# Scan layer: centring y from the first direction on, and ScalarE copying y into the opened PSUM sum

## Chip, cores and metric

The kernel runs on one core of one Trainium2 chip. The metric is the device time of one execution in microseconds (us). In this document TensorE is PE in the profile, its weight loads PEld, VectorE is DVE, ScalarE is ACT, GpSimd is POOL and the sync engine is SP.

## What is computed

Four layers run one after the other on 8 images of 64 channels and 64 x 64 pixels. Only the first, the scan layer, is touched. Per image it normalises and projects the input, convolves it, and runs a selective scan over the 4096 pixels in four directions k (along rows, along columns, and both backwards) with 16 states n per inner channel:

```python
def step(h, inp):
    u_t, dt_t, B_t, C_t = inp
    h = h * jnp.exp(dt_t[..., None] * A) + dt_t[..., None] * B_t[:, :, None, :] * u_t[..., None]
    return (h, jnp.einsum('bkcn,bkn->bkc', h, C_t))
...
y = out_y[:, 0] + inv[:, 0] + wh + invwh
y = _ln(y, outnorm_g, outnorm_b, LN_EPS) * jax.nn.silu(z)
```

Each `out_y` also has `D * xs` added, which is the input u scaled by channel. y is the sum of the four directions. `_ln` subtracts the mean over the 128 inner channels, and divides by the root of the variance.

## The kernel before, in words

`scan_layer` keeps the 128 inner channels on the partitions and cuts the 4096 pixels into 4 chunks of 1024 (`CH`), each two PSUM banks of 512 (`BK`) wide. An image is 16 steps: 4 directions by 4 chunks. The document numbers them by place, 0 to 15. All 8 images make 128 steps in one stream. A step is 16 units, one for each state n.

A unit is made of these instructions, in calls that run ahead of one another:

- `load` (L729, queued on SP) brings the row of C for this state, spread over 128 partitions, into a `ct` buffer (5 buffers). For units 0, 3, 6 and 8 (`BY_POOL`) the row of B comes likewise into `bt`.
- `decay` (L733): ScalarE's exponential a, 3 buffers.
- `spread`: z in PSUM (2 buffers). For the units in `BY_POOL` POOL multiplies bt (L741) and ScalarE copies it to PSUM (L748); for the other 12 TensorE spreads a bf16 row by two products (L751), and DVE multiplies (L778).
- DVE's scan h (L782, 3 buffers), then POOL's product of ct with h, in place in ct (L787).
- `sum_up` (L848): TensorE adds ct into the sum `yps`, two products of 512 columns in f32. The program's weights for this are `ctl["mat"]`: the identity up to place 10, and `lno_cen` (identity less 1/128 everywhere, which takes off the mean over channels) from place 11 on.

Sums come 3 units late (`LAG`). The instruction order on every engine is written out by hand in the loop over n at the end of `scan_layer`: `empty`, `spread(n + 1)`, then at n = 3 `bg.before` and `begin_sum`, at other n `sum_up` (twice at n = 7) and `bg.before`; then the loads, `decay(n + 2)`, `save_state` (L769, ScalarE copies one column), `product`, `unit(n)`, and `bg.after`. `bg` is the background queue: it interleaves the normalisation, projections and convolution (L544) of other steps and images, one piece per unit. `bg.before` issues the TensorE part of a piece, `bg.after` first all that was handed to `bg.later`, then the evacuation of the piece before (L647 and L648, for example).

The sum `yps` has one buffer of two banks. When the last unit of a step has been added, `empty` (L817), at n = 3 of the next step, lets ScalarE copy the sum to y in SBUF, and `begin_sum` opens the next one:

- at places 0 to 3 (`new_y`) by a product of u with `skipd`, the diagonal of the summed D;
- at places 4 and 12 the sum of the place before is kept (the direction turns on the same chunk), and nothing is opened;
- at the other ten by a product of the y that is there with `ctl["mat"]` (L839).

So 80 of the 128 steps open their sum from y: the "y steps". At the last four places the weights `lno_cen` centre both the y that is read back and the last direction, so that y is centred when `norm_y` takes its squares.

Of the kernel before, what the change touches and what calls it, by code (L numbers as in the profile page):

```python
# [11 lines left out]
BF16 = mybir.dt.bfloat16  # L12
AF = mybir.ActivationFunctionType
ALU = mybir.AluOpType
# [8 lines left out]
BK = 512  # L23
NBK = L // BK
DI = 128
N = 16
R = 4
CH = 1024
NCH = L // CH
# [212 lines left out]
def scan_layer(cm, x_in, w, xh):  # L242

    tc, nc = cm.tc, cm.nc
    with ExitStack() as ctx:
# [34 lines left out]
        for k in range(4):  # L280
# [5 lines left out]
            ps = psum.tile([128, BK], F32, name="wps", tag="mm")  # L286
# [14 lines left out]

        skip = cm.tile([DI, 1], "skip")
        nc.vector.tensor_reduce(skip, dcol, AX.X, ALU.add)
        skipd = cm.tile([DI, DI], "skipd")
        nc.vector.tensor_scalar(skipd, cm.ident, skip, None, ALU.mult)
        ln1_cen, ln1_avg = cm.tile([2 * C, 2 * C], "ln1_cen"), cm.tile([2 * C, 2], "ln1_avg")
        nc.vector.memset(ln1_cen, 0.0)
        nc.vector.memset(ln1_avg, 0.0)
# [6 lines left out]
            ln1_row, cm.ident[:NBK, :NBK].unsqueeze(2).to_broadcast([NBK, NBK, C])  # L315
        )
        lno_cen, lno_avg = cm.norm_consts(DI, "lno")

        eps = cm.tile([128, 1], "eps")
        nc.vector.memset(eps, 1e-5)  # L320
# [3 lines left out]
            rows, cm.ident[: 3 * N, : 3 * N].rearrange("p (i n) -> p n i", n=N), AX.X, ALU.add  # L324
        )
        nc.vector.tensor_copy(pick, rows)
        pad = padp.tile([DI, S + 2, S + 2], F32, name="pad", tag="pad")
        nc.gpsimd.memset(pad, 0.0)
        bg = Background()
# [272 lines left out]
        def ordered(t, k, c):  # L602

            if k % 2 == 0:
                return t[:, bass.ts(c, CH)].rearrange("p (a b) -> p a b", b=S)
            q = CH // S
            return t.rearrange("p (h w) -> p w h", w=S)[:, c * q : (c + 1) * q, :]
# [73 lines left out]
        def pieces(ctl, low):  # L681

            by_place = "a n (j x) -> (n j) a x"

            def fetch():
                low["b"] = work.tile([128, 2, 128], F32, name="bw", tag="bw", bufs=1)
                nc.sync.dma_start(low["b"], low["bc"][:, :N].rearrange(by_place, x=128))

            def first():
                low["p"] = work.tile([128, 3, 2, 128], BF16, name="bp", tag="bp", bufs=1)  # L690
                nc.scalar.copy(low["p"][:, 0], low["b"])

            def subtract():
                low["r"] = work.tile([128, 2, 128], F32, name="br", tag="br", bufs=1)
                nc.gpsimd.tensor_tensor(low["r"], low["b"], low["p"][:, 0], ALU.subtract)

            def second():
                nc.scalar.copy(low["p"][:, 1], low["r"])

            def third():  # L700
                nc.gpsimd.tensor_tensor(low["p"][:, 2], low["r"], low["p"][:, 1], ALU.subtract)

            def store():
                low["bsd"] = dr.tile([2, 3 * N, CH], BF16, name="bsd", tag="bsd", bufs=8)
                for i in range(3):
                    nc.sync.dma_start(
                        low["bsd"][:, i * N : (i + 1) * N].rearrange(by_place, x=128),
                        low["p"][:, i],
                    )

            def get():
                ctl["bs"] = work.tile([3 * N, CH], BF16, name="bs", tag="bs")
                nc.sync.dma_start(ctl["bs"], low["bsd"][ctl["k"] // 2])

            return ([fetch, first, subtract, second, third, store] if ctl["k"] < 2 else []) + [get]
# [77 lines left out]
        def layout(b, name):  # L793

            im = images[b]
            if name not in im:
                first = ("row", "col")[steps(b)[0][0] % 2]
                if name != first:
                    bg.flush(b - 1)
                at = b % 2 if name == first else 1 - b % 2  # L800
                im[name] = io.tile([DI, L], F32, name="y", tag=f"y{at}", bufs=1)
            return im[name]

        def own(t, c):
            return t[:, bass.ts(c, CH)].rearrange("p (a b) -> p a b", b=S)
# [18 lines left out]
        def begin_sum():  # L824


            ctl = pending[0][0]
            if kept:
                ctl["ps"] = kept.pop()
                return  # L830
            ctl["ps"] = psy.tile([DI, CH], F32, name="yps", tag="yps")
            half = BK // S
            if ctl["new_y"]:
                wt, so = skipd, ordered(ctl["u"], ctl["k"], ctl["c"])
            else:
                mine = ("row", "col")[ctl["k"] % 2]
                wt, so = ctl["mat"], own(layout(ctl["b"], mine), ctl["c"])
            for i in range(CH // BK):
                nc.tensor.matmul(  # L839
                    ctl["ps"][:, bass.ts(i, BK)].rearrange("p (a b) -> p a b", b=S),  # L840
                    wt, so[:, i * half : (i + 1) * half, :], start=True, stop=False,
                )

        def sum_up():

            ctl, n, ct = pending.popleft()
            for i in range(CH // BK):
                nc.tensor.matmul(  # L848
                    ctl["ps"][:, bass.ts(i, BK)], ctl["mat"], ct[:, bass.ts(i, BK)],
                    start=False, stop=(n == N - 1 and not ctl["turns"]),  # L850
                )
            if n == N - 1:
                if ctl["turns"]:
                    kept.append(ctl["ps"])
                else:
                    full.append(ctl)

        def steps(b):


            out = []
            for k in (0, 2, 1, 3) if b < NB - 1 else (1, 3, 0, 2):
                cs = range(NCH) if k < 2 else range(NCH - 1, -1, -1)
                out += [(k, c, i) for i, c in enumerate(cs)]
            return out
# [3 lines left out]
        def prepare(b, s):  # L869

            if b not in images:
                return None
            u = images[b]["u"]
            k, c, i = steps(b)[s]
            ks = [steps(b)[q * NCH][0] % 2 for q in range(4)] + [0]
            q = s // NCH
            bg.finish(b, 2 * c + 2 if s < NCH and k == 0 else NBK)
            low = lows.setdefault((b, k % 2, c), {}) if k < 2 else lows.pop((b, k % 2, c))
            dt, ut, e, items, soft = project(u, k, c, low)
            if b == 0 and s < NCH:  # L880
                items = later.pop(s, []) + items + [(None, soft[0]), (None, soft[1])]
            bg.add(items, first=True)
            new = work.tile([DI, N], F32, name="state", tag="state", bufs=3)
            ctl = dict(
                b=b, k=k, c=c, u=u, into=("row", "col")[ks[q + q % 2]], dt=dt, bc=low["bc"][k // 2], ut=ut, dus=e, soft=soft, new=new, state=None,
                first=(i == 0), new_y=(s < NCH), turns=(s % (2 * NCH) == NCH - 1),
                mat=lno_cen if s >= 3 * NCH - 1 else cm.ident,
            )
            ctl["pieces"] = pieces(ctl, low)
            return ctl  # L890
# [20 lines left out]
        with tc.manual_schedule():  # L911
            start(0)
            bg.drain()
            ctl = prepare(0, 0)
            bg.drain()
            ctl["soft"][2]()
# [10 lines left out]
            for b in range(NB):  # L927
                for s in range(4 * NCH):
# [3 lines left out]
                    if s + 1 < 4 * NCH:  # L932
                        nxt = prepare(b, s + 1)
                    else:
                        nxt = prepare(b + 1, 0)
# [22 lines left out]
                    for n in range(N):  # L958
# [3 lines left out]
                        if n == LAG + 1:  # L962
                            bg.before(n in idle, slots)
                            begin_sum()
                        else:
                            if len(pending) > LAG:
                                sum_up()
                            if n == LAG + 5:
                                sum_up()
                            bg.before(n in idle, slots)  # L970
# [22 lines left out]
                        if late and n == LAG + 2:  # L993
                            c = 4 * NCH - s
# [7 lines left out]
                    ctl = nxt  # L1002
            save_state()
            while pending:
                sum_up()
# [1152 lines left out]
```

## Time and profile before

| what | us |
|---|---|
| median of 3 runs (12318.48 to 12333.17) | 12329.48 |
| the profiled execution | 12328.75 |
| its span, first to last instruction | 12326.7 |
| first scan begins, last scan ends | 94.4, 7018.6 |
| POOL ct L787, 2048 instructions | 4794.6 busy, 2364 ns each |
| TensorE sums L848, 8192 records | 630 ns mean each |
| openings from y L839, 320 records | 592 ns median each |
| mean granted TensorE clock | 0.952 |

A row of groups reads: line, engine, operation, output and inputs by name, shape, count; then busy time in us and mean ns of one; then the engine's idle time just before these instructions, and what ended it. A product in f32 shows as two records of MATMUL, two passes; so 4096 sums of 512 columns are 8192 records. TensorE's records overlap their successors, so its busy share is no measure of how full it is. In a timeline the first two columns are start and duration, and square brackets hold the idle time before the instruction and what ended it. A row of waits gives us in total, times, and the longest.

### The profile page before, as it was taken

How to read it: one execution, taken by the hardware profiler on the slowest of the kernel's cores; microseconds unless marked ns; L12 is line 12 of the kernel's file. 1: busy time of each engine (PE TensorE's matmuls, PEld its weight loads, DVE VectorE, ACT ScalarE, POOL GpSimd, SP SyncE). 2: the span in 40 equal slices, each digit the busy share in tenths (PEclk: the TensorE clock that was granted, in tenths of full speed). 3: DMA queues.
4: the chain of work that ended last, by engine and by line, in shares of the span. 5: the costliest groups of instructions: out<-in, count | busy, mean ns of one | idle time of the engine just before them, and what ended most of it. 6: DMA issues, size and time to landing. Idle time of an engine off the chain costs nothing. (4 is left out here: it accounts for less than half of the span.)

```text
span 12326.7 us, 120038 instructions
## 1 busy us (share of the span) xinstructions
PE 11203.1 (91%) x38827; PEld 4075.9 (33%) x38827; DVE 10359.2 (84%) x7334; ACT 7820.8 (63%) x10409; POOL 7399.3 (60%) x3510
## 2 busy tenths in 40 slices
PE   7899999999999999999998899999987779999999
PEld 2233332332332332333322233232335463333333
DVE  5999999999999999999999776868677686676767
ACT  4776776776766766767766554646547574555554
POOL 5999999999999999999999700000006480000000
PEclk8999999999999999999999899999998789999999
DMA  3666666666666666666666400000011100000000
GB/s 115 207 213 218 209 209 217 219 203 216 218 210 213 211 210 217 213 215 213 199 213 211 164 24 26 5 25 7 17 41 41 41 21 24 19 4 19 5 11 6
DMA packets 541331, 1562.16 MB, mean 127 GB/s; under 512 B 127360, under 2 KB 144400, under 8 KB 538128
## 3 DMA queue, kind: packets, MB, share of 16 engines
q1 hardware_dynamic: 540688, 1554.36, 38.5%
q8 instruction: 309, 5.06, 0.2%
q14 instruction: 334, 2.74, 0.1%
HBM read 1456.41 MB, written 88.87 MB: 125 GB/s over the span
## 5 line engine op out<-in xcount | busy, mean ns | idle before, releaser
L787 POOL TENSOR_TENSOR ct<-ct,h 128x1024 f32<-128x1024 f32 x2048 | 4794.6, 2364 | 248.2 <-DVE h L782 113.3
L782 DVE TENSOR_TENSOR_SCAN h<-a,state,z 128x1024 f32<-128x1024 f32 x1536 | 3573.1, 2342 | 118.2 <-ACT z L748 67.1
L1159 DVE TENSOR_TENSOR sum<-sum,ex 128x1024 f32<-128x1024 f32 x1920 | 2347.5, 1223 | 618.1 <-ACT ex L1152 484.4
L1152 ACT ACTIVATE ex<-sc 128x1024 f32<-128x1024 f32 x2048 | 1968.1, 1024 | 1359.6 <-PE sc L1147 1359.6
L848 PE MATMUL yps<-ct,ident 128*128 128x512 f32 x5632 | 2809.0, 630 | 2.5 <-POOL ct L787 2.4
L733 ACT ACTIVATE a<-dt,amat 128x1024 f32<-128x1024 f32 x2048 | 2345.4, 1147 | 725.9 <-DVE h L782 712.5
L778 DVE TENSOR_TENSOR z<-z,e 128x1024 f32<-128x1024 f32 x1536 | 1863.3, 1213 | 221.1 <-PE z L751 143.2
L1166 PE MATMUL av<-ex,v 128*64 128x512 f32 x8192 | 1950.0, 604 | 0.0
L1147 PE MATMUL sc<-q,k 16*128 16x512 f32 (+1 forms) x8192 | 1562.2, 623 | 4.2 <-ACT q L1140 3.1
L848 PEld LDWEIGHTS yps<-ct,ident 128*128 128x128 f32 x5632 | 1006.4, 194 | 1384.2 <-issue 1220.6
L751 PE MATMUL z<-bs,pick 48*128 48x512 bf16 x3072 | 948.0, 389 | 536.5 <-DVE h L782 485.5
L848 PE MATMUL yps<-ct,lno_cen 128*128 128x512 f32 x2560 | 1276.3, 630 | 0.0
L782 DVE TENSOR_TENSOR_SCAN h<-a,z 128x1024 f32<-128x1024 f32 x512 | 1162.7, 2282 | 81.4 <-ACT z L748 57.2
L741 POOL TENSOR_TENSOR bt<-bt,e 128x1024 f32<-128x1024 f32 x512 | 1210.1, 2364 | 5.3 <-DMA bt<-bc 5.3
L1473 POOL TENSOR_TENSOR gt<-gt,pad 128x1024 f32<-128x1024 f32 x16 | 34.9, 2179 | 1570.2 <-ACT gt L1472 1570.2
L1166 PEld LDWEIGHTS av<-ex,v 128*64 128x64 f32 x8192 | 512.2, 136 | 1332.8 <-issue 1278.9
L1147 PEld LDWEIGHTS sc<-q,k 16*128 16x128 f32 (+1 forms) x8192 | 528.4, 184 | 1016.2 <-issue 977.3
L748 ACT COPY z<-bt 128x1024 f32<-128x1024 f32 x512 | 519.8, 1015 | 537.5 <-POOL bt L741 334.8
L751 PEld LDWEIGHTS <-pick 48*128 48x128 bf16 x3072 | 177.6, 95 | 1754.9 <-DVE h L782 1003.0
L848 PEld LDWEIGHTS yps<-ct,lno_cen 128*128 128x128 f32 x2560 | 458.1, 193 | 618.3 <-issue 564.2
L544 PE MATMUL vps<-pad,convd 128*128 128x512 f32 x1152 | 550.9, 602 | 12.9 <-ACT e L648 12.9
L1846 DVE RECIPROCAL r<-e 128x512 f32<-128x512 f32 x128 | 420.7, 3323 | 0.0
(416 smaller groups left out, 10449.5 us busy)
## 6 DMA issues: line engine op xcount, KB each, us to landing
ct<-bc SPq DMA_DIRECT2D x2048, 512.0 KB
bt<-bc SPq DMA_DIRECT2D x512, 512.0 KB
x<-x SPq DMA_DIRECT2D x12, 2048.0 KB
bc<-e SPq DMA_DIRECT2D x128, 128.0 KB
zd<-z SPq DMA_DIRECT2D x64, 256.0 KB
z<-zd SPq DMA_DIRECT2D x64, 256.0 KB
x<-x SPq DMA_DIRECT2D x32, 512.0 KB
part<-x SPq DMA_DIRECT2D x128, 128.0 KB
```

Of the source, the lines that this page charges most:

```text
L544: nc.tensor.matmul(held[0].rearrange("p (r c) -> p r c", c=S), convd[:, t, :], pad[:, j * rows + dy : (j + 1) * rows + dy, dx : dx + S], s ...
L733: ctl["exp", n] = nc.scalar.activation(ctl["a", n], ctl["dt"], AF.Exp, scale=amat[:, ctl["k"], n : n + 1])
L741: nc.gpsimd.tensor_tensor(bt, bt, ctl["dus"], ALU.mult)
L751: nc.tensor.matmul(z[:, bass.ts(i, BK)], pick[:, n : n + 1].to_broadcast([3 * N, DI]), ctl["bs"][:, bass.ts(i, BK)], start=True, stop=True,)
L778: first = nc.vector.tensor_tensor(z, z, ctl["dus"], ALU.mult)
L782: nc.vector.tensor_tensor_scan(h[:, flip], a[:, flip], z[:, flip], 0.0 if state is None else state[:, n : n + 1], ALU.mult, ALU.add,)
L787: freed[at] = nc.gpsimd.tensor_tensor(ct, ct, h, ALU.mult)
L848: nc.tensor.matmul(ctl["ps"][:, bass.ts(i, BK)], ctl["mat"], ct[:, bass.ts(i, BK)], start=False, stop=(n == N - 1 and not ctl["turns"]),)
L1147: nc.tensor.matmul(sc[:, e, :], k[r : r + d, bass.ts(j, 128)], qs[i][r : r + d, :], start=True, stop=True,)
L1152: nc.scalar.activation(ex, sc, AF.Exp)
L1159: nc.vector.tensor_tensor(sums[i], sums[i], ex, ALU.add)
L1166: nc.tensor.matmul(avs[i][r, :], v[:, j, r], ex[:, e, :], start=(j == 0), stop=(j == TQ - 1))
```

## The change

y is centred by every sum, not only from place 11 on: `skipd` is now the centring matrix times the summed D, `sum_up` always has the weights `lno_cen`, and `ctl["mat"]` is gone. What a y step reads back is therefore centred already and needs no product. Such a step opens its two banks with two products of a bf16 row of zeros (`nil`, 1 partition by 512), which make 128 x 512 zeros each, and ScalarE then copies y, 128 x 1024 f32, from SBUF over them. The copy is handed to `bg.later`, so it is issued at the end of n = 3, after the exponential of unit 5 and `save_state`. The sums that follow add to it.

```diff
-        skipd = cm.tile([DI, DI], "skipd")
-        nc.vector.tensor_scalar(skipd, cm.ident, skip, None, ALU.mult)
...
         lno_cen, lno_avg = cm.norm_consts(DI, "lno")
+        skipd = cm.tile([DI, DI], "skipd")
+        nc.vector.tensor_scalar(skipd, lno_cen, skip, None, ALU.mult)
...
+        nil = cm.pool.tile([1, BK], BF16, name="nil", tag="nil")
+        nc.vector.memset(nil, 0.0)
...
-            if ctl["new_y"]:
-                wt, so = skipd, ordered(ctl["u"], ctl["k"], ctl["c"])
-            else:
+            if not ctl["new_y"]:
                 mine = ("row", "col")[ctl["k"] % 2]
-                wt, so = ctl["mat"], own(layout(ctl["b"], mine), ctl["c"])
+                y = layout(ctl["b"], mine)
+                for i in range(CH // BK):
+                    nc.tensor.matmul(
+                        ctl["ps"][:, bass.ts(i, BK)], nil[:, :DI], nil, start=True, stop=False
+                    )
+                bg.later(lambda: nc.scalar.copy(ctl["ps"], y[:, bass.ts(ctl["c"], CH)]))
+                return
+            so = ordered(ctl["u"], ctl["k"], ctl["c"])
             for i in range(CH // BK):
                 nc.tensor.matmul(
                     ctl["ps"][:, bass.ts(i, BK)].rearrange("p (a b) -> p a b", b=S),
-                    wt, so[:, i * half : (i + 1) * half, :], start=True, stop=False,
+                    skipd, so[:, i * half : (i + 1) * half, :], start=True, stop=False,
                 )
...
-                    ctl["ps"][:, bass.ts(i, BK)], ctl["mat"], ct[:, bass.ts(i, BK)],
+                    ctl["ps"][:, bass.ts(i, BK)], lno_cen, ct[:, bass.ts(i, BK)],
...
-                mat=lno_cen if s >= 3 * NCH - 1 else cm.ident,
```

## The prediction, made before the result was known

> **What bounds the kernel now.** I began with the page's busy table and its 40 slices.
>
> ```profile
> PE 11203.1 (91%) x38827; PEld 4075.9 (33%) x38827; DVE 10359.2 (84%) x7334; ACT 7820.8 (63%) x10409; POOL 7399.3 (60%) x3510
> PE   7899999999999999999998899999987779999999
> DVE  5999999999999999999999776868677686676767
> ACT  4776776776766766767766554646547574555554
> POOL 5999999999999999999999700000006480000000
> ```
>
> POOL's digits are nines in the first 22 slices alone: that is the scan layer. Its first scan starts at 94 us and its last ends at 7018.6, so 128 steps take 54.1 us each. Nothing outside it changes. Next, the groups of instructions restricted to 94 to 7020 us, and the waits of the same stretch.
>
> ```profile
> L787 POOL TENSOR_TENSOR ct<-ct,h 128x1024 f32<-128x1024 f32 x2048 | 4794.6, 2364 | 248.2 <-DVE h L782 113.3 <-DMA ct<-bc 79.0 <-PE dps L619 16.6
> L778 DVE TENSOR_TENSOR z<-z,e 128x1024 f32<-128x1024 f32 x1536 | 1863.3, 1213 | 221.1 <-PE z L751 143.2 <-POOL ct L787 24.5 <-ACT u L553 15.1
> L748 ACT COPY z<-bt 128x1024 f32<-128x1024 f32 x512 | 519.8, 1015 | 537.5 <-POOL bt L741 334.8 <-DVE h L782 170.1 <-DVE z L778 14.9
> ...
> PEld yps L839 <- ACT y L817: 58.6, 72, 2.6
> ```
>
> By the stretch table POOL is busy 6676 of those 6926 us (96%), DVE 6549, ScalarE 4899. POOL is the bound; only its idle time can be won. I sorted its gaps over 0.06 us by unit and by kind of step. The 80 steps that open their sum from y (places 5 to 11 and 13 to 15 of each image's 16; in places 4 and 12 the sum is kept, 0 to 3 open from u) hold 125 us of POOL idle, 100 of it ahead of units 4 to 9. Why there, the timeline of one such step (place 14 of the third image) shows:
>
> ```profile
> 2630.06 0.19 ACT L769 COPY state<-h 128x1 f32<-128x1 f32 x1
> 2630.41 1.88 PE L839 MATMUL yps<-y,lno_cen 128*128 128x512 f32 x4
> 2632.22 0.60 PE L751 MATMUL z<-bs,pick 48*128 48x512 bf16 x2
> 2632.75 1.98 PE L848 MATMUL yps<-ct,lno_cen 128*128 128x512 f32 x4
> 2632.96 1.23 DVE L778 TENSOR_TENSOR z<-z,e 128x1024 f32<-128x1024 f32 x1 [0.48 <-PE z L751]
> 2638.58 2.36 POOL L787 TENSOR_TENSOR ct<-ct,h 128x1024 f32<-128x1024 f32 x1 [0.85 <-DMA ct<-bc]
> 2642.09 2.37 POOL L787 TENSOR_TENSOR ct<-ct,h 128x1024 f32<-128x1024 f32 x1 [1.16 <-DMA ct<-bc]
> ```
>
> The opening product (L839), z of unit 5 (L751), the first sum (L848), and then sums and convolution pieces follow on TensorE without a gap for 16 us. A sum releases its ct buffer; the load of a later ct waits for that buffer; POOL waits for the load. So in these steps TensorE's place in time after the opening is POOL's idle time. Place 9 agrees: the same step of different images takes 51.9 us where the opening begins 0.5 us after scan 3's end, 53.5 at 2.0, and 54.9 at 3.5.
>
> **What the skill says.** "PSUM — Partial Sum Buffer", section on the matmul accumulator, rule 2: ScalarE's writes leave the has_written bits alone, and a matmul without the first flag adds only where the bit is set. That is why two matmuls by zeros must open the banks; no trace here tests it. "TensorE: Matmul & The Clock Gate", Part 1: the clock is full or half, decided in free-running windows of 3.413 us. The trace agrees: in the scan the granted clock takes only the values 1 and 0.5, changes on a grid of 3.413 us, and is at half for 452 us. I set each window's streaming time beside the next window's clock: of 86 full-clock windows streaming under 45%, 81 were followed by half clock; of those over 60%, one of 1693. "ScalarE: Activation LUTs", section on what a table load costs: an immediate-scale activation takes 186 ns + 0.833 ns per element, 1039 ns for 1024, against 1015 in the L748 row.
>
> **Part by part, per y step.**
>
> TensorE loses 2 f32 products of 512 columns. Each is two passes, 0.43 us start to start in the timeline: 4 x 0.43 = 1.71 us. It gains two bf16 products of 1 row by 512 columns. Not in the trace; nearest is z (48 rows, 512 columns, bf16), 0.23 us start to start. Bounds 0.21 and, at half clock, 0.43 each; I take 0.22, so 0.43 for both, and 0.65 until the result is seen (0.60 for the z pair in its row, plus a semaphore). z of unit 5, queued behind, comes 1.28 us earlier unless scan 3 still holds its buffer.
>
> ScalarE gains one 128x1024 copy from SBUF to PSUM: the L748 row is that shape and direction, 1.015 us; bounds 1.0 and 1.15 (the L733 exponential). 80 x 1.03 = 82 us on ScalarE. It stands in its queue behind the exponential of unit 5 and state copy of unit 2 (L769), ahead of the background's evacuation (L647, L648 in that step) and the exponential of unit 6. It waits for the zero products; meanwhile those instructions wait too. Cover: after L769, ScalarE's idle time up to unit 8's z copy plus that copy's lead over scan 8 is 2.3 to 8.6 us in the 80 steps; copy and wait need 1.03 (1.9 or less in nine of ten, 4.1 at most), and the least margin is 0.8 us. For unit 6, reckoned alike, it is 0.15. So zero; if that cover were gone the copies would cost up to 82 us.
>
> **The added wait.** The first sum (L848) now waits for the copy. Behind it on TensorE stand the background product, sums 1 and 2, z of unit 7, the double sum; all that POOL's loads wait for. So the first sum's new start is the later of z 5 issued (opening + 0.95) and copy done + 0.06, with copy done = later of (L769's end, opening + 0.65) + 1.03. In the step shown: the opening starts at 2630.41, so the copy would end at 2630.41 + 0.65 + 1.03 = 2632.09 and the sum start at 2632.15 instead of 2632.75: 0.60 earlier. I did this for all 80 steps, and set against it what POOL idled ahead of units 4 to 9, since POOL can't gain more than it idles (means of 8 images, us):
>
> ```
> place      5    6    7    8    9    10   11   13   14   15
> advance   1.50 0.40 0.60 0.60 0.56 0.61 0.71 0.56 0.71 0.52
> POOL idle 0.87 0.26 0.50 0.43 0.77 0.93 3.25 1.59 1.94 1.95
> smaller   0.70 0.08 0.22 0.13 0.25 0.35 0.67 0.53 0.67 0.44
> ```
>
> "Smaller" is taken step by step before averaging. It sums to 32.5 us; the advances alone to 54. What is late next where the stall shrinks is the same ct load, only less, or POOL's own work.
>
> **The rest.** The sums of places 0 to 10 change weights from ident to lno_cen: 630 ns in both rows, 0. skipd is built a few DVE instructions later and nil is a memset of 512 elements on one partition; DVE idles 12.3 us soon after, before its reciprocal, and skipd is first used at 104.6 us: 0. No DMA is moved. SP's and POOL's orders are untouched.
>
> **Sum.** The profiled execution took 12328.75 us (span 12326.7 and 2.05 around it), within 0.8 us of the median, 12329.48. 12329.5 - 32.5 = 12297.
>
> **Rivals.**
>
> *POOL's work hides it.* POOL is busy 96%, and an earlier ct load may only uncover the next limit: DVE's results, of which it waits 113 us in the scan, or unit 9's load behind the double sum. For it: places 6 to 8 show next to no reachable idle. Against: places 11 to 15 wait 0.85 to 1.7 us for DMA several times in a row. If a quarter remains: -8 us, 12321.
>
> *Half clock* (the other side). The opening loses 1.28 us of streaming, 37% of a window, and TensorE now idles between z 5 and the copy's end. A window that falls under about 45% halves the next: 3.41 us streaming half as much, 1.71 us late, in just those sums POOL waits for. For it: place 5 already has 1.3 such windows per step, all y steps 0.36; whether products of one row count as activity no row shows. Against: shifting the grid over the streaming times with the change put in, I find 0.20 steps with a low window against 0.18, since background products fill TensorE right before the opening. It decides from 32.5 / 1.71 = 19 more such windows on. With 40, half a window per step: +68 - 32.5 = +36, 12365.
>
> *ScalarE comes late.* If z 8 or the step size (L653, L656) is late by half the copy in each step: +41 - 32.5 = +9, 12338. Against: the cover above.
>
> **Chances.** Forecast 0.58 (12275 to 12316), POOL hides it 0.21, half clock 0.15, ScalarE 0.06. About 0.2% (25 us) is what a measurement can tell from no change. Of the forecast's 0.58 some 0.45 lies beyond 25 us, with 0.02 of the others: faster 0.47. Slower is half clock and a little of ScalarE: 0.16. The rest, 0.37, is within. Range: below, all advances count (54) and some half windows vanish (about 12): 12263; above, into the half-clock case at about 30 windows, +20: 12350; some 0.08 of chance lies beyond each end.
>
> **What would show it.** Right: in the y steps POOL's idle ahead of units 4 to 9 falls from 100 us to about 68; DVE's wait for z L751 (143 us) falls; the new copies take about 1.03 us; the first sum waits for the copy 0.5 to 1 us in most steps; half clock stays near 452 us. Wrong: half clock over 500 us; POOL idle unchanged though the first sums are earlier; a new DVE wait for ScalarE's z or a.

## The result, and the profile after

The changed kernel takes 12349.25 us (median of 20 runs), against 12332.27 for the kernel before in the same number of runs: a ratio of 1.0015, 95% interval 1.001 to 1.0021. That is about 18 us slower, where 32 us faster was forecast: inside the stated range of 12263 to 12350 us, but on the wrong side of no change, which the interval excludes. Of all executions below one, of e9, ran in a much slower state (25855 us, mean granted clock 0.481), and no ratio counts it.

Executions of one kernel scatter, those of the changed kernel from 12330 to 12373 us, so one profile shows better where time goes than how much. The profiled execution of the changed kernel has a span of 12347.8 us, and its scan layer alone is 25 us longer than in the profile before: the last scan ends at 7044.0 us, not 7018.6.

The code after has moved down by two to seven lines: POOL's product is L789, the sums L855, DVE's z product L780, ScalarE's z copy L750. New are the zero products L839 and the copy L842. From the page of the changed kernel, the busy table and the slices:

```profile
PE 11169.4 (90%) x38667; PEld 4050.9 (33%) x38667; DVE 10362.7 (84%) x7335; ACT 7890.5 (64%) x10489; POOL 7398.9 (60%) x3510
POOL 5999999999999999999999800000006480000000
```

POOL's own work is the same to a microsecond, so the added time is POOL's idle time. The groups of the changed kernel between 94 and 7045 us:

```profile
L789 POOL TENSOR_TENSOR ct<-ct,h 128x1024 f32<-128x1024 f32 x2048 | 4791.1, 2360 | 274.4 <-DVE h L784 129.2 <-DMA ct<-bc 85.2 <-PE z L753 19.6
L855 PE MATMUL yps<-ct,lno_cen 128*128 128x512 f32 x8182 | 4144.3, 638 | 61.3 <-ACT yps L842 57.0 <-POOL ct L789 4.3
...
L780 DVE TENSOR_TENSOR z<-z,e 128x1024 f32<-128x1024 f32 x1536 | 1864.3, 1214 | 234.4 <-PE z L753 138.4 <-POOL ct L789 24.1 <-ACT state L771 15.6
...
L842 ACT COPY yps<-y 128x1024 f32<-128x1024 f32 x80 | 81.5, 1018 | 28.7 <-PE yps L839 27.7
```

The first row's idle time has risen from 248.2 to 274.4 us, though TensorE has less to do. The last row is the copy as it was costed: 1.018 us, 81.5 in all. The second row has the added wait, 57.0 us, and one more thing: a sum's record lasts 638 ns on average where it lasted 630. The median is 592 ns in both, so more of the sums ran at half clock. The granted clock says the same: in the scan it is at half for 602 us, not 452; over the whole profile it is 0.946, not 0.952. This is no accident of two profiles: the mean clocks of the 20 executions of the changed kernel lie between 0.943 and 0.948, those of 147 executions of the kernel before, timed beside the experiments, between 0.950 and 0.955. Behind the scan the clock is at half for 673 to 701 us in all 15 profiles, so it is in the scan that they differ. A step of 0.001 in the mean clock is 25 us of half clock.

What half clock costs at a bad spot, the start of place 7 in the fourth image shows. In the 17 us up to this point TensorE's instructions stand in the same order in both kernels, at the same distances to 0.02 us; only the edges of the windows fall elsewhere. First the changed kernel in the table of stretches, cut on the grid of 3.413 us:

```profile
3109.50:3112.91 3.41, 2.91 (x5) 1.04 (x6) 3.41 (x4) 2.34 (x4) 3.41 (x3) 0.50 0.65 227
3112.92:3116.32 3.40, 3.40 (x6) 0.87 (x5) 3.37 (x3) 1.81 (x3) 3.40 (x2) 0.50 0.13 49
3116.33:3119.74 3.41, 3.41 (x5) 0.96 (x4) 3.38 (x3) 2.18 (x3) 3.05 (x2) 0.50 0.27 102
```

The third number from the right is the clock: half, three windows long. The same units in the kernel before:

```profile
3102.77:3106.18 3.41, 3.41 (x6) 0.60 (x4) 3.37 (x4) 2.34 (x5) 3.41 (x2) 0.50 0.19 71
3106.18:3109.59 3.41, 3.41 (x8) 1.17 (x8) 3.37 (x3) 1.74 (x4) 3.41 (x3) 1.00 0.57 178
```

One window, then full clock. The changed kernel's timeline shows what follows at the opening of this step:

```profile
3116.65 0.34 PEld L855 LDWEIGHTS yps<-ct,lno_cen 128*128 128x128 f32 x1 [0.52 <-issue]
...
3122.55 1.92 ACT L819 COPY y<-yps 128x512 f32<-128x512 f32 x2 [1.34 <-PE yps L855]
...
3125.03 0.60 PE L839 MATMUL yps<-nil 1*128 1x512 bf16 x2
3125.73 1.02 ACT L842 COPY yps<-y 128x1024 f32<-128x1024 f32 x1 [0.24 <-PE yps L839]
3126.89 1.95 PE L855 MATMUL yps<-ct,lno_cen 128*128 128x512 f32 x4 [0.72 <-ACT yps L842]
3128.10 2.36 POOL L789 TENSOR_TENSOR ct<-ct,h 128x1024 f32<-128x1024 f32 x1 [1.10 <-DVE h L784]
```

The weight load of 0.34 us, 0.19 at full clock, is the sign of half clock. ScalarE's emptying copies wait 1.34 us for the last sum of the step before, everything behind them is late, and POOL idles. Place 7 takes 56.1 us after and 53.8 before (means of images 2 to 7); places 5, 9 and 11 take 0.6 to 1.0 us less than before.

The zero products of this step are not what makes these three windows: they come later, at 3125.03 us. The length of place 7 goes with where a window's edge falls. In the changed kernel, e3 and e12 (below) ten of these 18 steps are longer than 55 us, and those ten alone begin between 0.2 us before an edge and 0.6 us behind one. The changed kernel has five of them, e3 two, e12 three, the kernel before one. So a part of what this profile lost, 2.3 us in each of six steps, may be the chance of one execution; what the zero products themselves do to the clock, e3 shows.

### The profile page after: what moved, and what is told of

Its sections match the earlier page's. It is cut to its first block, busy times and chain, and to the rows that moved or that the text cites. A ratio compares the mean times of both kernels' runs of the same rounds, so it can differ in the third digit from the quotient of the medians.

```text
span 12347.8 us, 119848 instructions
## 1 busy us (share of the span) xinstructions
PE 11169.4 (90%) x38667; PEld 4050.9 (33%) x38667; DVE 10362.7 (84%) x7335; ACT 7890.5 (64%) x10489; POOL 7398.9 (60%) x3510
## 5 line engine op out<-in xcount | busy, mean ns | idle before, releaser
L789 POOL TENSOR_TENSOR ct<-ct,h 128x1024 f32<-128x1024 f32 x2048 | 4791.1, 2360 | 274.4 <-DVE h L784 129.2
L855 PE MATMUL yps<-ct,lno_cen 128*128 128x512 f32 x8192 | 4148.6, 638 | 61.3 <-ACT yps L842 57.0
L1158 ACT ACTIVATE ex<-sc 128x1024 f32<-128x1024 f32 x2048 | 1967.9, 1024 | 1359.8 <-PE sc L1153 1359.8
L855 PEld LDWEIGHTS yps<-ct,lno_cen 128*128 128x128 f32 x8192 | 1487.4, 196 | 2101.6 <-issue 1829.0
L780 DVE TENSOR_TENSOR z<-z,e 128x1024 f32<-128x1024 f32 x1536 | 1864.3, 1214 | 234.4 <-PE z L753 138.4
L750 ACT COPY z<-bt 128x1024 f32<-128x1024 f32 x512 | 519.7, 1015 | 499.8 <-POOL bt L743 295.8
L1855 POOL TENSOR_TENSOR r<-r,half 128x512 f32<-128x512 f32 x128 | 162.7, 1271 | 362.1 <-issue 188.0
L771 ACT COPY state<-h 128x1 f32<-128x1 f32 x2048 | 361.5, 177 | 4.7 <-DVE h L784 4.7
```

What stands on the lines that cost most here:

```text
L780: first = nc.vector.tensor_tensor(z, z, ctl["dus"], ALU.mult)
L789: freed[at] = nc.gpsimd.tensor_tensor(ct, ct, h, ALU.mult)
L855: nc.tensor.matmul(ctl["ps"][:, bass.ts(i, BK)], lno_cen, ct[:, bass.ts(i, BK)], start=False, stop=(n == N - 1 and not ctl["turns"]),)
L1158: nc.scalar.activation(ex, sc, AF.Exp)
```

## The experiments

Each was timed in alternation with the kernel before; ratios are to that kernel. "Half clock" is the sum over the scan in the profiled execution, where three kernels with the same TensorE work for the opening (before, e1, e2) gave 452, 476 and 435: differences under 40 us say nothing.

**e1, the centring alone.** `skipd` is centred as in the change; the other edits are:

```diff
...
-                wt, so = ctl["mat"], own(layout(ctl["b"], mine), ctl["c"])
+                wt, so = cm.ident, own(layout(ctl["b"], mine), ctl["c"])
...
-                mat=lno_cen if s >= 3 * NCH - 1 else cm.ident,
+                mat=lno_cen,
```

> Only the centring: every sum has the weights lno_cen and skipd is centred, but the y steps open by a product with the identity as before; no zero products, no ScalarE copy, no new wait. Clock theory (the zero products of one row and TensorE's new waits leave windows with too little activity, so the clock is halved more often): none of that is here, so half clock in the scan stays near 452 us and the time near the kernel before, 12332 +- 8 us. Weights theory (dense weights in all sums cost something): 12349 us, with half clock near 602.

Measured: 0.9996 (0.9988 to 1.0004), 12327 us, half clock 476. No cost of the dense weights shows.

**e2, ScalarE's load alone.**

```diff
+            if not ctl["new_y"]:
+                y = layout(ctl["b"], mine)
+                idle_copy = work.tile([DI, CH], F32, name="idle_copy", tag="idle_copy", bufs=1)
+                bg.later(lambda: nc.scalar.copy(idle_copy, y[:, bass.ts(ctl["c"], CH)]))
```

> The kernel before with one thing added: in each y step ScalarE makes the same 128x1024 copy of y at the same place of its queue, but into an SBUF tile that nobody reads; the opening product stays on TensorE. ScalarE theory (82 us more on ScalarE come late for DVE): at least 12349 us, since nothing is won on TensorE to set against it. Clock theory: ScalarE's cover holds, 12332 to 12338 us, half clock near 452 us.

Measured: 0.9996 (0.9988 to 1.0004), 12325 us. From the groups of e2 between 94 and 7013 us:

```profile
L846 ACT COPY idle_copy<-y 128x1024 f32<-128x1024 f32 x80 | 84.2, 1053 | 0.0
```

84 us of copies on ScalarE, and no time: the cover holds. These copies wait for nothing, where those of the changed kernel waited 28.7 us.

**e3, zeros on 128 partitions.**

```diff
-        nil = cm.pool.tile([1, BK], BF16, name="nil", tag="nil")
+        nil = cm.pool.tile([DI, BK], BF16, name="nil", tag="nil")
```

> The changed kernel with nil on 128 partitions in place of 1: the same two zero products, the same durations, the same waits. Clock theory, if activity counts rows: the windows with an opening are no longer low, half clock in the scan falls from 602 to about 500 us, and the time to about 12335 us. If rows don't count for activity, or if ScalarE or the weights are to blame: 12349 us and half clock near 600.

Measured: 0.9993 (0.9987 to 1.0), 12322 us, half clock 487. That is better than the 12335 us expected. One number in a tile's shape, with order, waits and values unchanged, is worth 27 us (1.0015 less 0.9993). The groups of e3 between 94 and 7013 us, to set beside those of the changed kernel:

```profile
L789 POOL TENSOR_TENSOR ct<-ct,h 128x1024 f32<-128x1024 f32 x2048 | 4794.2, 2363 | 241.3 <-DVE h L784 106.2 <-DMA ct<-bc 80.9 <-PE dps L621 18.5
L855 PE MATMUL yps<-ct,lno_cen 128*128 128x512 f32 x8182 | 4097.1, 632 | 61.4 <-ACT yps L842 54.5 <-POOL ct L789 5.3 <-POOL bt L743 1.4
```

POOL's idle time is down from 274 to 241 us and the mean sum from 638 to 632 ns, with the same wait for the copy: that wait, 54.5 us, is not what made the changed kernel slow.

Two openings that are alike in all but the rows show the step itself. In the changed kernel it is place 8 of the second image:

```profile
1464.28:1467.69 3.41, 2.80 (x9) 0.67 (x8) 3.41 (x3) 3.23 (x5) 3.41 (x2) 1.00 0.72 250
1467.69:1471.10 3.41, 2.86 (x4) 1.34 (x5) 3.38 (x3) 3.41 (x7) 3.41 (x3) 0.50 0.13 49
...
1466.38 0.60 PE L839 MATMUL yps<-nil 1*128 1x512 bf16 x2
1468.24 3.37 PE L855 MATMUL yps<-ct,lno_cen 128*128 128x512 f32 x4 [0.68 <-ACT yps L842]
```

In e3 it is place 8 of the third image:

```profile
2301.44:2304.85 3.41, 2.68 (x8) 0.79 (x8) 3.41 (x3) 3.34 (x5) 3.41 (x2) 1.00 0.92 256
2304.85:2308.26 3.41, 3.12 (x8) 1.48 (x9) 3.38 (x3) 3.41 (x7) 3.41 (x3) 1.00 0.09 23
...
2303.29 0.59 PE L839 MATMUL yps<-nil 128*128 128x512 bf16 x2
2305.14 1.96 PE L855 MATMUL yps<-ct,lno_cen 128*128 128x512 f32 x4 [0.58 <-POOL ct L789]
```

In both, TensorE streams for half of the first window without the zero products, and they add an eighth. With 1 row the next window is at half clock, and the four passes of the first sum take 3.37 us; with 128 rows it stays at full clock, and they take 1.96.

**e8 and e10, zeros on 32 and 64 partitions**, the same edit with another number.

> e3 with nil on 32 partitions. If activity is counted in proportion to the rows: the opening counts a quarter of what it does in e3, half clock 560 to 600 us and 12340 to 12350 us, nearly as with 1 row. If any product of a full row group counts whole: as e3, half clock near 490 and 12322 us.

> e3 with nil on 64 partitions. 1 row gave a ratio of 1.0015 and half clock 602 us, 32 rows 1.0013 and 551, 128 rows 0.9993 and 487. If activity is counted in proportion to the rows: 520 us of half clock and a ratio about 1.0005, 12336 us. If there is a threshold of rows, it is as one of the ends: 0.9993 or 1.0014.

Measured: 32 rows 1.0013 (1.0004 to 1.0021), half clock 551; 64 rows 0.9998 (0.999 to 1.0007), half clock 562. The traces say more than the times. I took the windows at full clock that hold a zero product, reckoned TensorE's streaming time in them without those products, and looked at the clock of the window after:

```
rows of the zero products                          1     32    64    128
windows with zero products, at full clock          83    80    80    77
... of them followed by half clock                 29    19    16    12
streaming without the products 45 to 50%           20    16    18     9
... of them followed by half clock                 14     4     0     0
streaming without the products 50% or more         48    47    43    50
... of them followed by half clock                  1     0     0     0
```

Just above the limit, where the products decide, 14 of 20 windows fall with 1 row, 4 of 16 with 32, none with 64 or 128. (The windows that the table leaves out stream under 45% without the products, and most of them fall with any number of rows: 14 of 15, 15 of 17, 16 of 19, 12 of 18.) So a product of one row, though it occupies TensorE for as long as one of 128, hardly counts as activity, and one of 128 does, zeros though its data are.

The mean clock over all executions puts the kernels in the same order: 0.9458 with 1 row, 0.9471 with 32, 0.9496 with 64, 0.9499 with 128 (20, 13, 13 and 22 executions). By it the 562 us of the profile with 64 rows are on the high side for that kernel. Between 64 and 128 rows no difference shows in time or clock; whether the count rises in proportion or by steps stays open.

**e12 and e13, bare weight loads against activity.** e9 (below) had shown a second cost of few rows: a product with another number of rows starts about 0.1 us later, because its weight load isn't hidden. From the background's last pass to z of unit 5 is 2.24 us in the kernel before, 1.06 in the changed one and with 32 rows, 0.96 in e3, 0.97 with 64 rows (medians at full clock, where nothing else stands between). e12 adds to e3

```diff
+                nc.tensor.matmul(
+                    ctl["ps"][:, :1], nil[:1, :DI], nil[:1, :1], start=False, stop=False
+                )
```

and e13 opens by two products of 1 row and adds two of 128 rows.

> e3 with one product of 1 row by 1 column of zeros behind its two zero products: activity as in e3, but one more change of the number of rows on TensorE. In e3's trace the product after a 128-row pass starts 0.43 us later, in the changed kernel the 1-row one 0.52 us later, so a change leaves about 0.1 us of weight load bare. If the bare weight loads are what made the changed kernel slow: back to a ratio of 1.0013 or more, 12345 us. If uncounted activity is: as e3, 0.9993 to 0.9998, 12322 to 12328 us.

> The changed kernel's two zero products of 1 row, followed by two of 128 rows into the same banks: the activity of e3 comes back, with 0.43 us more of TensorE time per y step and as many bare weight loads as the changed kernel or one more. If uncounted activity made it slow: half clock near 490 us and below the changed kernel, 12325 to 12335 us, in spite of the added work. If bare weight loads or TensorE time did: 12350 us or more.

Measured: e12 0.9995 (0.9987 to 1.0003), with the same distance as the changed kernel, 1.06 us, and half clock 490. The bare weight load doesn't explain the loss. e13: 1.0008 (1.0 to 1.0017), half clock 535, between the two expectations. Its copy comes after four products, and the first sum starts 0.42 us later than in e3 (mean of the y steps), so it doesn't separate the two. It does put a price on a late first sum: 0.42 us in 80 steps are 34 us, and it is 18 us slower than e3 (1.0008 less 0.9993).

**e4, e7 and e9, filling TensorE.** Ahead of each of the last five sums of a step:

```diff
+            if n >= 11:
+                for i in range(CH // BK):
+                    nc.tensor.matmul(
+                        ctl["ps"][:, bass.ts(i, BK)], nil[:, :DI], nil, start=False, stop=False
+                    )
```

e4 is e3 with it, e7 the kernel before with it and nil on 128 partitions, e9 the same with 1 partition.

> e3 with TensorE filled: ahead of each of the last five sums of every step (units 11 to 15) two more bf16 zero products of 128 rows are added into the same open sum, 0.43 us each time, 2.2 us per step of TensorE work that changes no value. Clock theory: half clock, which peaks at units 0 and 1 in both kernels, falls below 300 us in the scan, and the time to 12320 us or less. ScalarE or weights theory: 12349 us or, for the added work, more.

> The kernel before with e4's filling alone (two zero products of 128 rows ahead of each of the last five sums of a step). Clock theory in its strong form (half clock costs the kernel before time as well): half clock falls from 452 to about 300 us and the time to 12320 us or less. Weak form (half clock costs only where it falls on sums that POOL waits for, and 2.2 us per step of TensorE work costs as much as it wins): 12325 to 12340 us.

> e7 with the filling's zero products on 1 row in place of 128: the same TensorE time, the same order, no other difference. Clock theory: products of one row don't count, so half clock stays near the 452 us of the kernel before, or above, where e7 had 326, and the time is above e7's 12365 us: 12375 us or more. If only TensorE's time counts: 12365 us.

Measured: e4 0.9998 (0.9991 to 1.0004), half clock 319; e7 1.0029 (1.0019 to 1.004), half clock 326; e9 1.0082 (1.0069 to 1.0095), half clock 353. Half clock fell in e4 and e7, to a little more than the expected 300 us; the time did not follow. 2.2 us per step, 275 us in all, of added TensorE time cost the kernel before 36 us in spite of a better clock. This fits half clock being TensorE time in another form, which weighs only where POOL waits for what is late; no run takes the two apart.

Set against each other, e4 and e7 are the change itself, with zero products of 128 rows, at the same clock: the mean over their executions is 0.958 in both. e4's ratio is lower by 0.0031, or 38 us (some 23 to 53 by the two intervals; each was timed against the kernel before, on different chips). In their profiles the y steps take 42 us less and the other steps 2 us less. POOL's idle time ahead of units 4 to 9 falls from 110 to 77 us. So at an equal clock, and with TensorE fuller, the change wins about what was forecast.

e9's expectation on the time held, the one on the clock fell: half clock did not rise to 452 us. One row counts little here too: of the full-clock windows that only the added products lift over 45% streaming, 20 of 22 were followed by half clock, against none of 6 in e7 and 4 of 12 in e4. But low windows are fewer: without the added products 51 full-clock windows of e9 stream under 45%, 69 of e7. The reason for its time is in the starts. At full clock the pass behind a pair of 1-row products starts 0.30 us after the second, 0.22 with 128 rows, and the next pass 0.53 us later, 0.43 with 128 rows; ahead of the pair it is 0.52 against 0.43 where a 128-row pass stands there. That is about 0.2 to 0.3 us more for each of 640 pairs, 130 to 180 us of bare weight loads. That they keep TensorE late, so that it isn't idle where the clock would fall, fits the fewer low windows; no run tests it.

**e5, e6 and e11, an earlier first sum.** All on e3: e5 issues the copy at once in `begin_sum`, e6 calls `begin_sum` ahead of `bg.before`, e11 does both.

```diff
-                bg.later(lambda: nc.scalar.copy(ctl["ps"], y[:, bass.ts(ctl["c"], CH)]))
+                nc.scalar.copy(ctl["ps"], y[:, bass.ts(ctl["c"], CH)])
```

```diff
-                            bg.before(n in idle, slots)
                             begin_sum()
+                            bg.before(n in idle, slots)
```

> e3 with ScalarE's copy issued at once in begin_sum, ahead of the exponential of unit 5 and the state copy of unit 2, not after them. Theory that POOL waits for the first sum's start: the copy ends up to 1.3 us earlier where the state copy set it, the first sums of the y steps start earlier than in e3 by 0.5 us or so, and 12310 to 12316 us follow. Rival, that ScalarE's order matters more (the exponential of unit 5 comes 1 us or more late, and waits behind the zero products): no faster than e3, 12322 us or more.

> e3 with the opening ahead of unit 3's background product in TensorE's queue: that product then fills TensorE while ScalarE copies. Theory that TensorE's wait for the copy is what eats the gain: the wait nearly vanishes, first sums start earlier or equal, 12312 to 12318 us. Rival: the background product now waits with the opening for ScalarE's emptying copies, TensorE idles there and its chain is as late as before: 12322 us or more, half clock above e3's 487.

> e5 and e6 together, zero products on 128 rows: the opening ahead of unit 3's background product, and the copy ahead of unit 5's exponential. The earliest first sum that this order allows. If POOL's idle time follows the first sum's start: 12310 us or less. If it follows TensorE's load between the opening and the double sum, which is the same as in e3: 12318 to 12330 us.

Measured: e5 0.9992 (0.9984 to 1.0), e6 0.9999 (0.9991 to 1.0008), e11 1.0001 (0.9993 to 1.0009). The waits of e6 between 94 and 7006 us have

```profile
POOL ct L789 <- DMA ct<-bc: 88.5, 93, 4.6
PE yps L839 <- ACT y L819: 88.0, 72, 4.4
...
PE yps L855 <- ACT yps L842: 11.4, 21, 1.0
```

TensorE's wait for the copy is nearly gone, 11.4 us for 54.5, and nothing is won over e3. But the rival came in as well: the opening now waits 88.0 us for ScalarE's emptying copies, 23.0 in e3. So the first sum starts only 0.10 us earlier than in e3, in e5 0.12 and in e11 0.16, where 0.5 or so was expected. None of the three made the first sum clearly earlier, so they don't tell what that would be worth.

## Why the prediction was wrong

The starts in the y steps, in us after the end of scan 3 (means), and half clock and POOL's idle time in them (sums). 79 steps count; the last is left out, so POOL idles 97 us before, not 100. e1 and e2 open as the kernel before does, and show how far profiles with the same opening lie apart; e7 and e4 are the filled pair.

```
                                before    e1     e2    after    e3      e7     e4
z of unit 5                      2.69    2.74   2.48    1.40   1.37    2.82   1.27
first sum                        3.25    3.28   3.03    2.77   2.72    3.35   2.61
second sum                       5.98    5.96   5.74    6.00   5.62    6.03   5.48
third sum                        9.60    9.65   9.41    9.71   9.38    9.59   9.19
POOL's product of unit 7        16.12   16.23  16.00   16.23  16.02   16.19  15.84
half clock, units 0 to 3        172     179    139     200    186      84     60
half clock, units 4 and 5        44      31     30     118     71      18     55
POOL idle ahead of units 4 to 9  97     108     89     106     87     110     77
```

**The weights: right.** e1 is the same as before, within 10 us either way.

**The copy and its cover: right.** 1.018 us each; e2 shows the cover. DVE's scans wait 131.9 us for ScalarE's z in the changed kernel, 124.3 before and 112.2 in e3: nothing came late.

**The opening: right in size.** z of unit 5 comes 1.29 us earlier, 1.28 forecast. A change of rows adds 0.10 us per y step, which the prediction did not have and e12 shows to be harmless.

**The added wait: right but for a little.** TensorE waits 57.0 us in 77 of 80 steps, 0.74 each. The first sum starts 0.48 us earlier after and 0.53 in e3; the working had 0.68 (54 us over 80 steps).

**"Shifting the grid over the streaming times with the change put in, I find 0.20 steps with a low window against 0.18": this step failed.** It counted the zero products as activity for their whole time: the loss that it names, 1.28 us, is 1.71 less their 0.43. The prediction said that no row shows whether products of one row count, and then took them at full value all the same. They count for next to nothing: half clock rose by 150 us, 44 windows, where 19 were named as the point from which the half-clock rival decides. The table shows where: in units 4 and 5, right behind the opening, by 74 us. Half of that, 37 us over 79 steps, is 0.47 us more between first and second sum, and the first sum's 0.48 us is gone at the second. e3, which differs in the rows alone, keeps 0.36 of its 0.53 us there.

The rows are not the whole of it. In e3, where the products count, the mean clock of 22 executions is still 0.950 against 0.952 before, some 60 us of half clock or 17 windows, where 0.20 less 0.18 of 80 steps is about two. So the shifted grid was too hopeful even with full activity; why, no run shows.

The rival had the sign and the mechanism. Its price of 1.71 us for each window was too high as a mean. The 27 us between the changed kernel and e3 against 34 windows more in the profiles (602 less 487 us) make 0.8 each, and against 30 by the mean clocks 0.9. The scatter of the kernel before agrees: over its 147 executions the time falls by 6.5 us for each 0.001 of mean clock (correlation -0.77), which is 0.9 us a window; this is no experiment. At a bad spot the price is higher. Place 9, which the prediction read as the cost of a late opening, is one: its images with 51.9, 53.5 and 54.9 us have 3.4, 6.8 and 10.2 us of half clock up to scan 6, or 1.5 us for each window. That the time lies inside the range at all is in part luck: its upper end reckoned with 30 windows at twice the price, and 44 came.

**The sum of 32.5 us: nearer than the times show.** e3 wins 9 us (0 to 16), with a clock that is still lower than before. Put at an equal clock by the slope of 6.5 us for 0.001, an estimate that rests on the scatter alone, the changed kernel wins 23 us, e3 24, e5 and e10 20, e12 15; and e4 against e7 measures 38. In the other direction e13 lost 18 us by 34 us of later first sums. So some 0.4 to 0.6 of what the first sum moves seems to arrive at the end; the term "smaller of advance and POOL idle" counted 32.5 of 54 us, which is 0.6. Between 20 and 38 us the runs don't say whether it was too large.

Where the rest goes is only partly seen. The first sum's advance shrinks on the way: in e3 from 0.53 us to 0.22 at the third sum and 0.10 at POOL's product of unit 7, in e4 against e7 from 0.74 to 0.40 and 0.35. The rows of e1 and e2 say how far to trust this: profiles with the same opening lie up to 0.25 us and 19 us of POOL's idle time apart, so e3's last two steps and its 10 us less of POOL's idle time are within the spread. Two reasons are in the traces. Half clock in units 4 and 5 is still 27 us more in e3 than before, 0.17 us per step. And the third sum stands behind z of unit 7, which waits for scan 5: in 30 steps before and 26 in e3 that z starts within 0.25 us of scan 5's end, and scan 5 has moved by only 0.14 us. The rest is not settled.

**POOL hides it, and ScalarE comes late.** Of the first, this much is seen: a part of the advance doesn't arrive. That a quarter remains is not shown, since e3's 9 us hold the worse clock too. The second has e2 and the scans' waits against it.

Of the 26 us by which the scan layer is longer in the profile after, 9 lie in the y steps and 17 in the others, in which no zero product runs. The half clock of the others rose too, from 186 to 243 us (210 in e1 and in e2). But e1's y steps are 13 us longer than those of the kernel before, with the same opening, so one profile can't carry this split. That the other steps lose because they begin where the y steps left the windows' grid and TensorE's backlog is possible; no experiment took them apart.

## What to carry to other kernels

Work taken off TensorE can cost time where the clock follows activity: reckon for each window of 3.4 us what is left in it, and count products of few rows as little unless a run has shown otherwise (here the time was lost with 1 row and with 32). A placeholder product that only opens a bank can as well be made on 128 rows: here it took as long and kept more of the clock. Before the rest of a forecast is called wrong, compare kernels at an equal clock; the mean granted clock of every execution is on record, and tells more than the half clock of one profile. And before an advance at one instruction is booked as gain for another engine, follow it over the waits between them: here about half of it seems to have arrived.

## What was not expected of the hardware

A bf16 zero product by 512 columns takes the same 0.22 us start to start with 1, 32, 64 and 128 rows; its weight on the clock does not stay the same (14 of 20, 4 of 16, 0 of 18 and 0 of 9 windows at the limit were followed by half clock).

A change in the number of rows between products leaves about 0.1 us of weight load bare (0.52 us against 0.43 behind an f32 pass). From 64 rows to 48 there is none: z starts 0.22 us behind the 64-row zero product, 0.31 behind that of 128 rows, 0.31 behind that of 1 row.

At half clock it takes a larger share of the window to get out than it took to fall in: of the changed kernel's 177 half-clock windows all 26 that streamed 65 to 80% of their time were followed by another, and none of the 33 that streamed over 95%. The Trainium skill, "TensorE: Matmul & The Clock Gate", Part 1, has a busy window release the clock and an idle one take it away; here "idle" begins well above nothing. In streaming time at the clock of the moment, the limits are about 45% at full clock and 80 to 95% at half; since a column takes twice as long there, that is about the same number of columns in a window.

ScalarE's copy of 128x1024 f32 took 1018 ns into PSUM and 1053 into SBUF.
